# Moving the turning back of outputs, a set of score maxima and a norm between the gate steps of a gated feed-forward

## The chip, the cores and the metric

The kernel runs on one core of a Trainium2 chip. The metric is the device time of one execution, in microseconds (us); the time given for a kernel is the median of its runs.

## The reference

Two layers of a gated block work on eight sequences of 256 rows, 512 wide, with a context of 256 rows each. Cut to what matters:

```python
x = x + tanh(g_xattn[0]) * causal_attention(layernorm(x), ctx, ctx)      # 16 heads of 32
x = x + tanh(g_ffn[0]) * ffn0(layernorm(x))    # rms_norm(silu(gate) * up) @ w_proj, ternary weights
x = x + tanh(g_xattn[1]) * attention1(layernorm(x), ctx)   # projections, normed queries and keys
x = x + tanh(g_ffn[1]) * ffn1(layernorm(x))    # 8-bit activations, ternary weights
```

The change lies in the part that computes `ffn0` of layer 0 for all sequences, with the attention of layer 0 for the later sequences woven into it.

## The kernel before

The program has three parts. The first (until about 190 us) quantizes the weights of `ffn0`, computes keys and values for layer 1 and begins the attention of sequences 0 and 1. The second (about 190 to 728 us) runs `ffn0` of sequences 0 to 7 as eight blocks, b = 0 to 7. The third runs layer 1.

**A block.** `Feed0(b).chunks()` are 19 steps, one gate step to a sixteenth of the block's time. The last three project and overlap the next block's first three. A step n (called chunk n here) handles 128 rows and 256 hidden columns. TensorE (PE) computes `gu` in 32 matmuls. ScalarE (ACT) takes a tanh (L910) and VectorE (DVE) two products (L911, L912) that give `h` and free the PSUM bank of `gu`, of which there are two. ACT makes a half-precision copy (L916), DVE for even chunks or GpSimd (POOL) for odd ones the remainder `hs` (L299). ACT squares (L919), and POOL sums the squares into `acc` (L921). PE projects the chunk three steps later into `y` (one PSUM bank). After every eight chunks the row sum of squares `ssq` (PSUM tag `o`, one bank) gives a factor (L272 on DVE, L274 on POOL, L958 on DVE), and L963 adds `y` to the rows `x`.

**The feed-forward's entry.** `Feed0.ready()` has two steps. `norm` takes moments on DVE (L281, L282, L289, L272), `rs_r` on POOL (L274) and two normed tiles `y` on POOL (L294). `turn` casts the first `y` on ACT (L884), takes the remainder on DVE (L885) and issues a transposing DMA on the SP queue (L886), then does the same for the second. The tile `yp` between has one buffer:

```python
for i, y in enumerate(self.y):
    pp = f0.tile([P, 2, D], F16, tag="yp", name="yp", bufs=1)
    nc.scalar.copy(pp[:, 0], y)
    nc.vector.tensor_tensor(pp[:, 1], y, pp[:, 0], ALU.subtract)
    nc.sync.dma_start(out=self.xT[:, i], in_=pp.rearrange("p h d -> p (h d)"), transpose=True)
```

The first transposed half `xT[:, 0]` is read from chunk 0 of the sequence's block on, the second from chunk 8 on.

**The attention.** For the attention that is woven into block n (of sequence n + 2), `looks()` are four sets of scores with their negated maxima `nm` (L411, in layer 1 L419, on DVE), one set for four heads; then `parts`, which splits `nm` into three bf16 pieces `mz` in ten small POOL operations (L431, L434, L438); then `shift`, which turns `mz` on PE (`nt`) and copies it on DVE to `nT` (L449). `weighs()` computes the scores once more, adds `nT` in PSUM, takes exponentials `p` on ACT (L485) and multiplies by values (`o`, copied to `oT` by L519, sums on POOL by L522). `done()` turns the outputs back on PE (`back`, and `sums` in the PSUM bank `o`), inverts and multiplies on DVE (L584, two L590), and adds into `x` on DVE (two L600). `ready()` of the attention has a norm like the feed-forward's and `turn`, which turns `y` on PE (`turned`) with an ACT copy to `qT` (L348). Scores, `back`, `nt` and `turned` share a PSUM tag `s` of two buffers, two banks each.

**The weights of layer 1.** During blocks 0 to 2 ACT measures them (L1004). From about block 3 to 6 POOL scales and rounds them (L1028, L1032), DVE clips them (L1036) and SP stores them (L1037); loads are L993.

**What sets the order.** Every step has a place in time in blocks, written by hand: `at(b, (k, step))` places it at b + k/16, and `timeline` calls all steps by place. A step thus only emits its instructions in that order; the compiler's scheduler then orders them on each engine with a model of its own, and each engine runs its queue in order. PE's queue is held to the order of the calls (`pe.held`).

In block b, with the places in sixteenths, this stands between chunk 9 and the next block:

```
9.2   third scores; last weigh of the attention of sequence b + 1
10    chunk 10
10.4  fourth scores      10.8  parts
11    chunk 11
11.7  done (sequence b + 1: turn the outputs back, add to x)
12    chunk 12           12.4  feed-forward norm of sequence b + 1
13    chunk 13           13.4  feed-forward turn (casts, DMA)
14    chunk 14           14.6  shift (nt)
15    chunk 15           15.3  first exponentials
16    chunk 0 of block b + 1
```

Block 0 has `done` of sequence 1 at 1.3 and the feed-forward norm of sequence 1 at 4.4, outside this scheme. Blocks 5 and 6 also compute queries of layer 1 (`lin`) between chunks 12 and 14. In block 7 there is no `done` or norm for a next sequence.

Of the kernel before, what the change touches and what calls it, by code (L numbers as in the profile page):

```python
# [87 lines left out]
def flamingo_kernel(  # L88
# [39 lines left out]
    def banks(stack, name, **tags):  # L128
        pool = stack.enter_context(
            tc.tile_pool(name=name, bufs=1, space=PSUM, reuse_waits="tile")  # L130
        )
        part_ps.clear()
        part_ps.update({tag: (pool, n) for tag, n in tags.items()})
# [15 lines left out]
    def load_x(i, pool):  # L149
        xs[i] = pool.tile([P, D], F32, tag=f"x{i}", name=f"x{i}", bufs=1)  # L150
        nc.sync.dma_start(out=xs[i], in_=xf[i * P : (i + 1) * P, :])
# [44 lines left out]
    for g in range(DC):  # L196
        for i in range(2):
            at = SR * g + SR // 2 * i
# [163 lines left out]
    class Attention:  # L362
# [3 lines left out]
        n = 0  # L366
# [250 lines left out]
    def timeline(*jobs):  # L617

        steps = []
        for j, (a, z, job) in enumerate(jobs):  # L620
            steps += [(a + (z - a) * (n + 0.5) / len(job), j, step) for n, step in enumerate(job)]
        for _, _, step in sorted(steps, key=lambda e: e[:2]):
            step()

    def at(b, *steps):

        return [(b + n / 16, b + n / 16, [step]) for n, step in steps]
# [192 lines left out]
    with ExitStack() as part:  # L820
# [16 lines left out]
        jobs = []  # L837
# [162 lines left out]
    def measure1(u):  # L1000
        seen[0] += 1
        w = load1(u)
        a = q1.tile([P, QW], BF, tag="q", name="a1", bufs=2)
        behind(nc.scalar.activation(a, w, AF.Abs, accum_out=l1sum[:, u : u + 1]), block["A"])  # L1004
# [17 lines left out]
    def quantize1(u):  # L1022

        seen[1] += 1
        assert seen[0] == n1
        w = load1(u)
        _, dst, k = units1[u]
        ins = nc.gpsimd.tensor_scalar(w, w, wscale[:, k : k + 1], MAGIC, ALU.mult, ALU.add)  # L1028
        behind(ins, block["P"])
        hold1()  # L1030
        q = q1.tile([P, QW], BF, tag="q", name="q1", bufs=2)
        nc.gpsimd.tensor_scalar(q, w, 1.0, -MAGIC, ALU.mult, ALU.add)  # L1032

        def hold():
            q8 = q1.tile([P, QW], F8, tag="q8", name="q8", bufs=2)
            nc.vector.tensor_scalar(q8, q, 1.0, -1.0, ALU.min, ALU.max, saturate=False)  # L1036
            nc.sync.dma_start(out=dst, in_=q8.bitcast(U8))  # L1037

        left.append(hold)
# [83 lines left out]
    with ExitStack() as part:  # L1123
        banks(part, "ps1", o=1, gu=2, y=1)
        q1 = part.enter_context(tc.tile_pool(name="q1", bufs=1, side="right", reuse_waits="tile"))
        feed0 = [Feed0(b) for b in range(B)]

        def rows(b):
            load_x(2 * b, x2)
            load_x(2 * b + 1, x2)  # L1130

        jobs = [
            (0.5, 3.0, [lambda u=u: measure1(u) for u in range(n1)]),
            (3.05, 3.05, [scales1]),
            (3.1, 6.5, [lambda u=u: quantize1(u) for u in range(n1)]),
            (6.6, 6.6, [hold1]),
            (3.0, 3.0, [load_queries]),
        ]

        jobs += at(0, *zip((-5.0, -4.0), feed0[0].ready()), (1.3, *att0[1].done()))
        for b in range(B):
            jobs += at(b, *((k, step) for k, step in enumerate(feed0[b].chunks())))
            if b == 0:
                jobs += at(b, *zip((4.4, 5.4), feed0[1].ready()))
            elif b + 1 < B:
                jobs += at(b, *zip((12.4, 13.4), feed0[b + 1].ready()))
        for n, a in enumerate([*att0[2:], *att1[:2]]):  # L1150
            if n < B - 2:
                jobs += at(n, (-11.0, lambda n=n: rows(n + 2)))
                jobs += at(n, *zip((-4.8, *((1.4, 4.2) if n == 0 else (-2.4, 0.2))), a.ready()))
            else:
                jobs += at(n, *zip((-9.6, -7.6, -3.7, -2.6, -2.5, -2.4, 0.2), a.ready()))
            jobs += at(n, *zip((*((5.4, 7.2) if n == 0 else (1.2, 5.2)), 9.2, 10.4, 10.8, 14.6), a.looks()))
            if a is not att1[1]:
                jobs += at(n, *zip((15.3, 18.2, 19.2, 20.2, 22.2, 23.2, 24.2, 25.2), a.weighs()))
            if n < B - 2:
                jobs += at(n, (27.7, *a.done()))  # L1160
        timeline(*jobs)
    w0ctx.close()

# [197 lines left out]
    jobs = []  # L1361
    for b in range(B):
        first, second, a = feed1[2 * b], feed1[2 * b + 1], att1[b]
# [77 lines left out]
```

## Time and profile before

| | us |
|---|---|
| median of 3 runs (1191.4 to 1193.26) | 1191.43 |
| the profiled execution: its own time | 1192.33 |
| the profiled execution: span, first to last instruction | 1190.6 |
| PE busy (share of the span) | 1092.7 (92%) |
| DVE busy | 791.4 (66%) |
| ACT busy | 598.0 (50%) |
| POOL busy | 495.1 (42%) |

A line of the timeline gives the start and the length in us, the engine, the source line, the operation, the tile written and those read, partitions and shape, and in brackets the idle time before it and what ended that. A line of the waits gives who waited on whom: us in total, how often, the longest. A row of the windows gives a stretch, its length, the busy time of PE, PE's weight loads, DVE, ACT and POOL with instructions in parentheses, the granted TensorE clock, the DMA share and GB/s. One core runs, so its mean granted clock, 0.987, is the only one.

### The profile page before, as it was taken

How to read it: one execution, taken by the hardware profiler on the slowest of the kernel's cores; microseconds unless marked ns; L12 is line 12 of the kernel's file. 1: busy time of each engine (PE TensorE's matmuls, PEld its weight loads, DVE VectorE, ACT ScalarE, POOL GpSimd, SP SyncE). 2: the span in 40 equal slices, each digit the busy share in tenths (PEclk: the TensorE clock that was granted, in tenths of full speed). 3: DMA queues.
4: the chain of work that ended last, by engine and by line, in shares of the span. 5: the costliest groups of instructions: out<-in, count | busy, mean ns of one | idle time of the engine just before them, and what ended most of it. 6: DMA issues, size and time to landing. Idle time of an engine off the chain costs nothing.

```text
span 1190.6 us, 31314 instructions
## 1 busy us (share of the span) xinstructions
PE 1092.7 (92%) x13290; PEld 738.2 (62%) x13389; DVE 791.4 (66%) x1612; ACT 598.0 (50%) x1060; POOL 495.1 (42%) x792
## 2 busy tenths in 40 slices
PE   5899998999999989988999998998999999999987
PEld 1445446777777767776667775565656565656654
DVE  5686986745647375655656445687878787868585
ACT  3466554466665434344443542536363646464654
POOL 3112112543435475565645226544444444424250
PEclk9999999999999999999999999999999999999999
DMA  8444435523433233242311114011122122211212
GB/s 300 142 161 160 146 138 182 156 90 109 107 109 99 65 93 99 82 101 90 83 50 42 20 37 159 25 44 49 50 49 51 45 55 45 55 32 31 44 41 57
DMA packets 99469, 104.08 MB, mean 87 GB/s; under 512 B 60992, under 2 KB 72320, under 8 KB 99328
## 3 DMA queue, kind: packets, MB, share of 16 engines
q1 hardware_dynamic: 95728, 96.03, 27.8%
q10 hardware_dynamic: 3600, 6.03, 1.6%
q8 instruction: 105, 1.72, 0.6%
q14 instruction: 36, 0.29, 0.1%
HBM read 72.09 MB, written 15.73 MB: 74 GB/s over the span
## 4 chain that ended last, share of the span: by engine, by line
PE 34%; DVE 26%; POOL 17%; ACT 11%; issue 9%; DMA 3%; DVEq 0%; POOLq 0%; SPq 0%; ACTq 0%
PE gu L257 9%; PE o L257 6%; PE lin L257 6%; PE s L257 5%; DVE nm L419 4%; PE y L257 3%; ACT h L919 2%; POOL rs_r L274 2%; DVE h L912 2%; DMA xT<-yp 2%; DVE h L911 2%; PE py L257 2%; POOL hs L299 2%; POOL acc L921 2%; ACT hs L916 2%
## 5 line engine op out<-in xcount | busy, mean ns | idle before, releaser
L257 PE MATMUL gu<-xT,gu 128*128 128x128 f16 x4096 | 256.4, 222 | 10.5 <-DMA xT<-yp 6.8
L257 PEld LDWEIGHTS <-gu 128*128 128x128 bf16 x4096 | 238.9, 99 | 40.8 <-issue 18.0
L274 POOL TENSOR_TENSOR rs_r<-rs_t,mhalf 128x1 f32<-128x1 f32 (+1 forms) x88 | 61.9, 705 | 212.7 <-DVE rs_t L272 200.9
L257 PE MATMUL gu<-gv,zT 128*128 128x256 fp8e4 x1024 | 131.7, 275 | 6.0 <-ACT gv L1269 4.6
L921 POOL TENSOR_TENSOR acc<-acc,h 128x256 f32<-128x256 f32 x112 | 82.7, 739 | 114.9 <-ACT h L919 113.0
L257 PEld LDWEIGHTS <-zT 128*128 128x128 bf16 x1024 | 96.4, 98 | 51.8 <-issue 36.5
L1269 ACT COPY gv<-gu 128x512 f32<-128x512 f32 x128 | 74.0, 584 | 95.6 <-PE gu L257 75.3
L916 ACT CAST hs<-h 128x256 f16<-128x256 f32 x128 | 51.7, 404 | 138.7 <-DVE h L912 137.9
L257 PE MATMUL y<-pr,hs 128*128 128x512 bf16 x413 | 113.0, 381 | 6.2 <-DVE x L963 0.6
L485 ACT ACTIVATE p<-s 128x768 f32<-128x768 f32 (+1 forms) x128 | 109.5, 906 | 16.0 <-PE s L257 15.5
L911 DVE SCALAR_TENSOR_TENSOR h<-h,gu 128x256 f32<-128x256 f32 x128 | 53.2, 416 | 95.4 <-ACT h L910 95.2
L919 ACT ACTIVATE h<-h,hid 128x256 f32<-128x256 f32 x112 | 56.7, 508 | 67.4 <-POOL hs L299 41.3
L419 DVE TENSOR_REDUCE nm<-s 128x4 f32<-128x1024 f32 x64 | 75.7, 1219 | 21.8 <-PE s L257 21.8
L299 POOL TENSOR_TENSOR hs<-h,hs 128x256 f16<-128x256 f32 x64 | 43.7, 683 | 100.2 <-ACT hs L916 100.2
L1274 DVE SCALAR_TENSOR_TENSOR t<-t,gv 128x512 f32<-128x512 f32 x64 | 48.3, 754 | 45.9 <-ACT t L1273 45.9
L257 PE MATMUL s<-qT,kT 32*128 32x256 f32 (+1 forms) x1024 | 74.9, 372 | 2.6 <-DVE rs_t L272 1.6
L910 ACT ACTIVATE h<-gu 128x256 f32<-128x256 f32 x128 | 48.4, 378 | 50.4 <-PE gu L257 49.9
L257 PE MATMUL s<-kT,qT 32*128 32x256 f32 (+1 forms) x1024 | 68.9, 374 | 2.3 <-ACT p L485 1.9
L257 PE MATMUL lin<-wk,cT 128*128 128x512 f32 x128 | 61.0, 621 | 9.8 <-DMA wk<-in_k_wT_dram 9.8
L411 DVE TENSOR_REDUCE nm<-s 128x2 f32<-128x256 f32 (+1 forms) x128 | 62.8, 552 | 8.9 <-PE s L257 8.9
L257 PE MATMUL o<-p,v 128*32 128x256 f32 (+1 forms) x1024 | 61.7, 358 | 6.9 <-DVE x L1306 4.9
L522 POOL TENSOR_TENSOR oT<-oT 128x128 f32<-128x128 f32 x48 | 26.6, 555 | 98.4 <-ACT oT L519 98.4
(180 smaller groups left out, 2070.5 us busy)
## 6 DMA issues: line engine op xcount, KB each, us to landing
w<-in_gvT_dram SPq DMA_DIRECT2D x32, 512.0 KB
w<-in_guT_dram SPq DMA_DIRECT2D x16, 512.0 KB
w<-in_outT_dram SPq DMA_DIRECT2D x16, 512.0 KB
cT<-in_cxT_dram SPq DMA_DIRECT2D x8, 512.0 KB
x<-in_x_dram SPq DMA_DIRECT2D x16, 256.0 KB
kT<-in_cxT_dram SPq DMA_DIRECT2D x8, 512.0 KB
v<-in_cx_dram SPq DMA_DIRECT2D x8, 512.0 KB
kd<-k SPq DMA_DIRECT2D x8, 512.0 KB
```

The source lines that it names most:

```text
L257: return self.kept(nc.tensor.matmul(*args, **kwargs))
L274: nc.gpsimd.tensor_tensor(r[:, :n], t[:, :n], mhalf[:, :n], ALU.pow)
L299: (nc.vector if engine == "V" else nc.gpsimd).tensor_tensor(dst, a, b, op)
L411: nc.vector.tensor_reduce(nm[:, :, qb], s[j][:, :, at[qb] : at[qb] + to[qb]], AX.X, ALU.max, negate=True,)
L419: nc.vector.tensor_reduce(nm, s[j].rearrange("p r (q k) -> p r q k", q=2), AX.X, ALU.max, negate=True)
L485: exp[0] = nc.scalar.activation(self.p[j], s[j][:, :, 0:n], AF.Exp)
L910: block["A"] = nc.scalar.activation(h, gu[:, 0], AF.Tanh, scale=0.5 / UP0)
L911: nc.vector.scalar_tensor_tensor(h, h, 1.0, gu[:, 0], ALU.add, ALU.mult)
L916: nc.scalar.copy(hs[:, 0], h)
L919: nc.scalar.activation(sq, h, AF.Square, scale=hid[:, 1:2])
L921: block["P"] = nc.gpsimd.tensor_tensor(self.acc[i], self.acc[i], sq, ALU.add)
L1269: nc.scalar.copy(self.gv[:, :, k % 2, :], gu)
```

## The change

Places in time change, and nothing else. In blocks 1 to 6, `done` goes from 11.7 to 10.7, the feed-forward norm from 12.4 to 11.4 and its `turn` from 13.4 to 12.4. In all blocks the fourth scores go from 10.4 to 11.2 and `parts` from 10.8 to 11.6.

```diff
             elif b + 1 < B:
-                jobs += at(b, *zip((12.4, 13.4), feed0[b + 1].ready()))
+                jobs += at(b, *zip((11.4, 12.4), feed0[b + 1].ready()))
...
-            jobs += at(n, *zip((*((5.4, 7.2) if n == 0 else (1.2, 5.2)), 9.2, 10.4, 10.8, 14.6), a.looks()))
+            jobs += at(n, *zip((*((5.4, 7.2) if n == 0 else (1.2, 5.2)), 9.2, 11.2, 11.6, 14.6), a.looks()))
...
             if n < B - 2:
-                jobs += at(n, (27.7, *a.done()))
+                jobs += at(n, (26.7, *a.done()))
```

(The place 27.7 of the attention that is woven into block n is 11.7 of block n + 1.)

The order within a block is now: chunk 10, `done`, chunk 11, fourth scores, norm, `parts`, chunk 12, `turn`, chunk 13, chunk 14, `shift`, chunk 15.

## The prediction

> **What bounds the kernel now.** I read the page first: PE is busy 92% of the span, so time is lost only where PE stands still, and the list of what PE waited for comes next.
>
> ```profile
> PE gu L257 <- DMA xT<-yp: 6.8, 4, 2.8
> PE back L260 <- DVE nm L411: 1.0, 3, 0.3
> ```
>
> The first row is what the change can take away: four waits of the first gate matmuls of a block for the transposed rows `xT`. By window they are 0.93 us (block 1 into 2), 1.19 (2 into 3), 1.89 (3 into 4) and 2.79 (4 into 5). Blocks 5 and 6 show none. Next, PE's timeline where block 4 passes into block 5:
>
> ```profile
> 504.81 1.96 PE L257 MATMUL gu<-xT,gu 128*128 128x128 f16 x32 [0.55 <-DVE h L912]
> 507.47 0.28 PE L260 MATMUL nt<-ident_b,mz 128*128 128x128 bf16 x2
> 515.29 1.96 PE L257 MATMUL gu<-xT,gu 128*128 128x128 f16 x32 [2.79 <-DMA xT<-yp]
> 517.08 1.04 PE L260 MATMUL turned<-ident,y 128*128 128x128 f32 x8
> ```
>
> A gate step is 1.96 us of `gu` plus 0.8 to 1.0 of `y`. `nt` (the turned maxima) does not wait. Then POOL's timeline beside it:
>
> ```profile
> 498.06 0.20 POOL L431 TENSOR_SCALAR mz<-nm 128x16 bf16<-128x16 f32 x1
> 500.11 0.20 POOL L438 TENSOR_SCALAR mz<-nmr 128x16 bf16<-128x16 f32 x1
> 500.27 0.67 POOL L299 TENSOR_TENSOR hs<-h,hs 128x256 f16<-128x256 f32 x1
> 501.57 0.73 POOL L921 TENSOR_TENSOR acc<-acc,h 128x256 f32<-128x256 f32 x1 [0.62 <-ACT h L919]
> 502.27 1.55 POOL L1028 TENSOR_SCALAR w<-w,wscale 128x1024 f32<-128x1024 f32 x1
> 503.91 1.04 POOL L1032 TENSOR_SCALAR q<-w 128x1024 bf16<-128x1024 f32 x1
> 506.64 0.71 POOL L274 TENSOR_TENSOR rs_r<-rs_t,mhalf 128x2 f32<-128x2 f32 x1 [1.69 <-DVE rs_t L272]
> 508.04 1.52 POOL L294 TENSOR_SCALAR y<-x,ln_mv,rs_r 128x512 f32<-128x512 f32 x2
> ```
>
> The ten `mz`/`nmr` operations (`parts`) end at 500.3, so `nt` at 507.47 has 7.1 us of slack; the norm's `y` ends at 509.6. The chain of waits for this window runs through POOL, ACT and DVE in turn, not through PE. Last, ACT and DVE, where the transfer hangs:
>
> ```profile
> 510.13 0.68 DVE L885 TENSOR_TENSOR yp<-y,yp 128x512 f16<-128x512 f32 x1
> 515.26 0.62 ACT L884 CAST yp<-y 128x512 f16<-128x512 f32 x1 [2.83 <-DMA xT<-yp]
> 515.79 1.50 ACT L485 ACTIVATE p<-s 128x768 f32<-128x768 f32 x2
> ```
>
> `yp` has one buffer, so the second cast waits on ACT until the first transpose landed, 4.4 us after its issue at 510.84 (3.6 us in block 3). `turned` then takes the PSUM buffer that the first of the two `p` frees.
>
> **The change part by part.** Nothing is added or removed. In the built order of PE, `back`/`sums` and chunk 11 now stand ahead of the fourth scores in blocks 1 to 6; in blocks 0 and 7 only the scores go behind chunk 11. On DVE the four L411 leave their place ahead of the outputs' L584 to L600 and stand behind them and the first norm statistics. On POOL `parts` no longer stands ahead of hs(11): it comes behind hs(11) and acc(11), and it is cut in two by the norm's `rs_r` and its two `y`. That cut decides my forecast. I lay block 4 out again with the durations of before, PE reaching `back` at 493.2 as it then reached the scores.
>
> 1. `back` ends at 494.1. `sums` needs PSUM bank `o`, held by `ssq` until DVE reads it (L272, 494.45, behind an L1036): a new wait of 0.55. Behind it on PE stands chunk 11, 494.75 to 496.7, `y` to 497.6. The 0.34 of `back <- nm` is gone.
> 2. DVE is free for L584 at 496.62 (there the four L411 began). 0.39 and 1.20 for the two L590 give 498.2, which frees the buffer that the fourth scores need: PE waits 0.8, and chunk 12 starts at 499.4.
> 3. DVE goes on with L600 0.93, L911 0.45, L600 0.93, statistics 0.6, L912 0.45: the `h` of chunk 11 is done at 501.45, against 499.4. Chunk 12's `h` is done at 505.1 after statistics 0.6 and four L411 1.9, so chunk 14 starts at 505.15, 0.35 later than before.
> 4. POOL: hs(11) 502.0 to 502.65, ACT's square, acc 503.95, L1028 at 1.1 to 505.05, two `mz` 505.45, `rs_r` 506.15, L1032 507.2, two `nmr` 507.55, two `y` 509.05, acc 509.75, two `mz` 510.1, hs(13) 510.75, two `nmr` and two `mz` 511.6. PE is ready for `nt` at 507.95 and waits 3.7 us. Queued behind it are chunk 15, the first exponentials' scores and chunk 0: that starts at 516.65 against 515.29.
> 5. The transfer: first `y` 508.3 (0.5 earlier), cast on ACT 508.95, but DVE's L885 stands behind an L1036 that waits for L1032 (507.2), behind L911 and L912 of chunk 13 and behind two L281: 509.95 to 510.6. The issue on SP is 0.2 us earlier than before, not a step. It lands by 515.0, which the `nt` wait hides; the 2.79 is gone.
> 6. The second cast still blocks ACT until 515.0, now with chunk 15's tanh queued behind it. `p` also stands behind the square of chunk 15, which needs POOL's hs(15), which stands behind the attention norm: acc(13) 512.2, L1028 513.3, `rs_r` 514.4, acc 515.1, L1032 516.1, two `y` 517.6, hs(15) 518.3, square 518.85, first `p` read by 519.7. `turned` starts at 519.7 against 517.08: **+2.6**.
>
> Block 3 has the same rows 69.5 us earlier: `turned` at 450.2 against 447.88, **+2.3**. Blocks 1 and 2 have no L1028/L1032. There `parts` ends at 307.1 and `nt` waits 1.0; chunk 0 of block 2 starts at 312.1 (before 312.06, of which 0.93 waiting). POOL's attention norm is late (its L272 stands behind the copy of `nt`: 309.7, two `y` until 313.0), hs(15) 314.35, first `p` by 315.75: `turned` against 313.92 gives **+1.8**. Block 2 lies 62.5 us later: 378.25 against 378.06, **+0.2**, because the old 1.19 and a wait of 1.27 ahead of `turned` go. In blocks 5 and 6 two stretches of 3.6 us of `lin` lie ahead of `nt` and cover `parts`. Their new waits at `sums` and scores (1.35 in block 5, none in block 6), less two `back` waits of 0.3 and part of the 0.75 of `s <- nT`, are **+0.2**. In blocks 0 and 7 `parts` comes one step later (about 2.8 us) under some 5 us of cover: 0. Uncovered, that step would cost up to 2.8 each. In layer 1 PE's order is unchanged; stores and `uT` transposes change places on SP. The only wait there of `py` on `uT` is 2.4 us: I take 0, bounds -2 and +2.
>
> What a wait of 3.7 us does to the clock, rows of before bound:
>
> ```profile
> 444.80:448.00 3.20, 3.12 (x33) 3.12 (x34) 0.85 (x2) 2.53 (x4) 3.20 (x4) 0.59 0.14 30
> 515.20:517.00 1.80, 1.71 (x31) 1.72 (x32) 1.03 (x1) 1.74 (x3) 1.80 (x3) 1.00 0.00 0
> ```
>
> After the wait of 1.89 the granted clock (third number from the end) was 0.59, and 32 `gu` took 3.21 instead of 1.96; after the 2.79 it was 1.00. So the price is 0 or 1.25 per stall. I take 0, since `turned` waits until 519.7 anyway and chunk 0 would end at 519.9 with it.
>
> The Trainium skill, "TensorE: Matmul & The Clock Gate", section "What's actually happening", says that an idle window of about 3.4 us drops the clock to half. By it both 3.7 us waits would cool PE and the sum would be 2.5 higher; the row at 444.8 shows a drop after a shorter gap, so here the rows decide.
>
> Sum: 2.6 + 2.3 + 1.8 + 0.2 + 0.2 = **+7.1 us** on the profiled execution's 1192.33 (span 1190.6 and 1.7 around it) = 1199.4. That execution was 0.9 above the median 1191.43, so I predict 1198.5.
>
> **Rivals.** (a) Faster: the norm is early enough and `nt` finds its parts. For it: all four `xT` waits are under 2.8 us, less than one step. Against: POOL's order puts `y` into the middle of `parts`. It decides if the last `mz` of blocks 3 and 4 is done by 508, 3.6 us ahead of my layout. Then 6.8 and 0.7 of `back` waits go, less new waits at scores and `sums` of about 2.7: -4.8, 1186.6; down to 1184 without them. (b) No change: `nt` waits as laid out, but squares and `p` do not slip. Then `turned` moves with chunk 0: +1.4 and at most +2.3 in blocks 4 and 3, 0 and -1.5 in blocks 1 and 2, in all +1 to +2: about 1193. That is also what follows if the issue of `xT` moves by just 0.2. (c) Worse: the clock drops after both stalls and SP's new order holds up `uT`: +2.5 and +2, 1203.
>
> **How the numbers follow.** My layout 0.56, (a) 0.17, (b) 0.17, (c) 0.10. About 0.2% (2.4 us) is what a measurement of this kernel can tell from no change. Faster is (a), 0.17; same is (b), 0.17; slower is mine and (c), 0.66. The range goes from 1188, inside (a), to 1203.5, just above (c).
>
> **What would show it.** Right: PE's waits list `nt <- POOL mz`, about 1 us in blocks 1 and 2 and 3 to 4 in blocks 3 and 4; `gu <- xT` is gone; `turned <- ACT p` grows to 1 or 2 us a time; the first `xT` issue of block 4 comes no more than 1 us sooner against chunk 14. Wrong: `nt` without a wait, or a last `mz` ahead of the two `y`; then (a) holds.

## The result, and the profile after

The changed kernel takes 1209.07 us (median of 4 runs, 1208.45 to 1210.92) against 1191.51 for the kernel before: a ratio of 1.0153 with a 95% interval of 1.0137 to 1.0169. That is 17.6 us slower; the forecast was 7.1 slower. The direction was right, the size not, and the time lies above the range. The profiled execution has a span of 1207.6 us (before 1190.6).

First, what PE waited for (waits of PE, changed kernel; total us, times, longest):

```profile
PE nt L260 <- POOL mz L438: 10.7, 4, 4.2
...
PE gu L257 <- DMA zT<-zq: 3.4, 2, 2.0
...
PE s L257 <- DVE nT L449: 2.5, 2, 2.3
```

The first row is the predicted wait of the turned maxima; in order of time its four parts are 1.11, 1.11, 4.22 and 4.22. No row `gu <- DMA xT` is left, and none of `back`. Two rows the prediction had not foreseen: `s <- nT` was 0.7 and is 2.5, and `gu <- zT` in layer 1 was one wait of 1.3 and is two of 3.4 in all. (`sums <- rs_t`, which it had foreseen, is 1.4.)

PE's timeline where block 4 passes into block 5 (start, us, operation, and in brackets the wait ahead of it):

```profile
499.02 0.30 PE L260 MATMUL sums<-ident,oT 128*128 128x128 f32 x1 [0.61 <-DVE rs_t L272]
...
515.93 0.45 PE L260 MATMUL nt<-ident_b,mz 128*128 128x128 bf16 x2 [4.22 <-POOL mz L438]
516.17 3.53 PE L257 MATMUL gu<-xT,gu 128*128 128x128 f16 x32
...
524.50 1.06 PE L260 MATMUL turned<-ident,y 128*128 128x128 f32 x8
```

PE stands still for 0.61 us ahead of `sums`, as laid out (0.55), and for 4.22 us ahead of `nt`. Chunk 15 then takes 3.53 in place of 1.96, and `turned` comes at 524.50, 7.42 later than before. POOL's timeline beside it:

```profile
508.84 0.38 POOL L431 TENSOR_SCALAR mz<-nm 128x16 bf16<-128x16 f32 x2
509.18 0.71 POOL L274 TENSOR_TENSOR rs_r<-rs_t,mhalf 128x2 f32<-128x2 f32 x1
509.87 1.05 POOL L1032 TENSOR_SCALAR q<-w 128x1024 bf16<-128x1024 f32 x1
510.88 0.84 POOL L434 TENSOR_TENSOR nmr<-nm,mz 128x16 f32<-128x16 f32 x2
511.72 1.52 POOL L294 TENSOR_SCALAR y<-x,ln_mv,rs_r 128x512 f32<-128x512 f32 x2
...
515.67 0.37 POOL L438 TENSOR_SCALAR mz<-nmr 128x16 bf16<-128x16 f32 x2
```

This is the order that the prediction laid out: two `mz`, `rs_r`, L1032, two `nmr`, the two `y` of the norm, and the last `mz` at 516.0.

To see where the 17 us arise, I take the starts of the same PE operations in both traces, `turned` where a block ends and later `nt`, and note by how much the shift grows from one mark to the next:

| stretch | shift grows by | forecast |
|---|---|---|
| up to block 1 | -0.2 | 0 |
| block 1 / 2 / 3 / 4 | +1.24 / -0.16 / +2.78 / +3.74 | +1.8 / +0.2 / +2.3 / +2.6 |
| blocks 5 and 6, to `nt` of block 7 | +4.1 | +0.2 |
| from there into the second sequence of layer 1 (`turned` at 870.63) | +3.6 | 0 |
| from there to the last tile | +1.9 | 0 |

Blocks 1 to 4 give 7.6 of a forecast 6.9. The miss lies behind them: 4.1, 3.6 and 1.9.

### The profile page after: what moved, and what is told of

Read it like the earlier page. It is cut to its first block, busy times and chain, and to the rows that moved or that the text cites. A ratio compares the mean times of both kernels' runs of the same rounds, so it can differ in the third digit from the quotient of the medians.

```text
span 1207.6 us, 31403 instructions
## 1 busy us (share of the span) xinstructions
PE 1104.6 (91%) x13389; PEld 742.5 (61%) x13389; DVE 790.7 (65%) x1612; ACT 597.1 (49%) x1060; POOL 497.1 (41%) x792
## 4 chain that ended last, share of the span: by engine, by line
PE 34%; DVE 25%; POOL 19%; ACT 10%; issue 9%; DMA 2%; POOLq 0%; DVEq 0%; SPq 0%; ACTq 0%
PE gu L257 10%; PE lin L257 6%; PE o L257 6%; PE s L257 5%; DVE nm L419 4%; PE y L257 3%; POOL rs_r L274 3%; DVE h L912 2%; POOL acc L921 2%; ACT h L919 2%; POOL hs L299 2%; PE py L257 2%; DVE h L911 2%; POOL w L1028 2%; POOL q L1032 2%
## 5 line engine op out<-in xcount | busy, mean ns | idle before, releaser
L257 PE MATMUL y<-pr,hs 128*128 128x512 bf16 x512 | 132.5, 382 | 0.9 <-DVE x L963 0.9
L921 POOL TENSOR_TENSOR acc<-acc,h 128x256 f32<-128x256 f32 x112 | 81.8, 731 | 117.3 <-ACT h L919 110.2
L919 ACT ACTIVATE h<-h,hid 128x256 f32<-128x256 f32 x112 | 56.7, 507 | 71.6 <-POOL hs L299 46.0
```

The lines of the kernel that those rows point to most:

```text
L257: return self.kept(nc.tensor.matmul(*args, **kwargs))
L919: nc.scalar.activation(sq, h, AF.Square, scale=hid[:, 1:2])
L921: block["P"] = nc.gpsimd.tensor_tensor(self.acc[i], self.acc[i], sq, ALU.add)
```

## The experiments

The kernel before took 1191.0 to 1191.6 us (median) beside each of them. "By the marks" means the shift of the same PE operations against the trace of before.

**The parts alone.** The first run moves only the fourth maxima and the parts (against the kernel before):

```diff
-  9.2, 10.4, 10.8, 14.6), a.looks()
+  9.2, 11.2, 11.6, 14.6), a.looks()
```

> The fourth scores and parts stand behind chunk 11 as in the change; outputs, norm and turn stay where they were. On POOL parts is whole and ahead of the norm's two y, and the instructions of layer 1 stand in the order of before. Theory A (the loss in blocks 1 to 4 is POOL's cut parts, so that nt waits): no wait of nt over 1 us, the xT waits of 6.8 us stay, 1190 to 1195 us. Theory B (what costs is that the fourth scores and their maxima come late at all): nt waits 2 us or more in blocks 3 and 4 here too, 1198 us or more.

Measured 1213.77 us, ratio 1.0184 [1.0168, 1.0199]. `nt` does not wait, as theory A had it, but the time is 23 us up, a miss for both theories: `back <- nm` 6.1, `gu <- h` 7.4 and `y <- x` 5.3 are longer or new, and 3.3 of the `xT` waits stay. With the maxima late, the outputs and products behind them on DVE hold PE up, as POOL does in the whole change.

The second moves only the outputs and the norm:

```diff
-  (12.4, 13.4), feed0[b + 1].ready()
+  (11.4, 12.4), feed0[b + 1].ready()
-  (27.7, *a.done())
+  (26.7, *a.done())
```

> Outputs, norm and turn a step sooner; fourth scores and parts stay ahead of chunk 11. Both theories: nt does not wait, the xT waits are gone (-6.8 us). Price: back now stands right behind the fourth scores on PE and needs the PSUM buffer that their first two L411 free; by the rows of before these end 3.4 us after PE gets there in blocks 3 to 5 and 1.8 us in blocks 1 and 2, 2 in block 6, so back <- nm waits some 15 us in all. 1199 us, range 1190 to 1203.

Measured 1209.93, ratio 1.0156 [1.0137, 1.0175]. The wait is as expected:

```profile
PE back L260 <- DVE nm L411: 13.8, 5, 3.5
```

It is the largest of PE's waits in that trace, the `xT` waits are gone, and still the time is 11 us above the forecast and outside its range. The granted clock of PE, which the forecast did not count, goes with that: between block 1 and `nt` of block 7 its mean is 0.962 in this trace and 0.986 in that of before, which leaves out some 12 us more of PE's work (one minus the mean clock, times the length of the stretch). So the two halves cost about 23 and 19 us, and together 17.6: they partly undo each other, and no half is a gain.

**POOL's order alone.** The third run keeps the change, but the parts come at 11.3 and the norm's two `y` are held behind the last of them (against the changed kernel):

```diff
-  9.2, 11.2, 11.6, 14.6), a.looks()
+  9.2, 11.2, 11.3, 14.6), a.looks()
-  nc.gpsimd.tensor_scalar(y, t, ...)
+  behind(nc.gpsimd.tensor_scalar(y, t, ...), last_mz)
```

> The change, with the places of the scores and parts at 11.2 and 11.3 and the two y of the feed-forward's norm held behind the last operation of parts on POOL. The rest of the order of blocks 3 and 4 stays, but layer 1's instructions fall back into the order of before. Theory A: nt waits 1.6 us instead of 4.2 in blocks 3 and 4 and under 1 in blocks 1 and 2. For layer 1, theory C (its 5.5 us of loss come from the order of its instructions on DVE, POOL, SP): they go, 1196 us. Theory D (they come from entering layer 1 late or from the clock): they stay, 1201 to 1204 us.

Measured 1205.66, ratio 1.0114 [1.0097, 1.0132]:

```profile
PE turned L260 <- POOL acc L922: 6.0, 2, 3.5
...
PE turned L260 <- ACT p L486: 3.5, 3, 2.0
...
PE nt L260 <- POOL mz L439: 3.2, 2, 1.6
PE gu L257 <- DMA xT<-yp: 3.0, 3, 2.0
```

(The lines of this run are numbered one higher.) The waits for the multipliers fall from 10.7 to 3.2, so POOL's cut `parts` do make them. But 3.0 of `xT` come back and `turned` waits 9.5 in place of 3.2: by the marks the time up to `nt` of block 7 is longer than in the changed kernel (+14.4 against +11.5). POOL's work has to be done in either order. The time lies above the ranges of both C and D; by the marks C is right, as layer 1, back in the order of before, adds nothing behind that mark (-0.7).

**Blocks alone.** The change in some blocks, the old places in the others:

```diff
-  (11.4, 12.4), feed0[b + 1].ready()
+  (11.4, 12.4) if b in blocks else (12.4, 13.4), feed0[b + 1].ready()
-  9.2, 11.2, 11.6, 14.6), a.looks()
+  9.2, *((11.2, 11.6) if n in blocks else (10.4, 10.8)), 14.6), a.looks()
-  (26.7, *a.done())
+  (26.7 if n + 1 in blocks else 27.7, *a.done())
```

> The whole change in blocks 3 and 4 alone; blocks 0, 1, 2, 5, 6, 7 have the places of before. Layer 1's order is nearly that of the changed kernel. Theory A: nt waits 4.2 us twice, turned of the attention norm in block 5 comes 6.5 us late, as the changed kernel adds in these two blocks. Theory C: layer 1, from the nt of block 7 to the end, is 5 us longer than before, 472 us instead of 467. Together with 1.5 us of slow clock in block 5: 1204 us. Theory D says the same for a late entry, theory B the same for the blocks.

> The whole change, but in blocks 5 and 6 of layer 0 alone; layer 1 then has the instruction order of the kernel before. In the changed kernel the marks of the turned tiles go from +7.4 us at the end of block 4 to +11.5 us at the norm of block 7, so blocks 5 and 6 cost 4.1 us there. Theory A (these blocks cost by their own moved steps): about 4 us here too, 1195 us (1194 to 1197). Theory B (the cost is carried over from the waits of blocks 3 and 4, by the clock or a queue that is behind): nothing here beyond the 0.2 us of the prediction, 1191.5 us (1190.5 to 1192.5).

> The whole change in blocks 1 and 2 of layer 0 alone; layer 1 has the order of before. The prediction gave these blocks 2.0 us, the marks of the changed kernel 1.1 us (1.24 and -0.16). If blocks add up: 1192.5 us (1191.5 to 1193.5), with two waits of some 1.1 us of the norm's transposes for its multipliers. If what a block costs depends on the blocks around it: 1196 us or more, or below 1191.

> The whole change in blocks 1 to 4 of layer 0; blocks 5, 6, 0 and 7 keep the old places, and layer 1 has an order close to that of the changed kernel. All theories: +7.5 us at the end of block 4, with the four waits of the norm for its multipliers (1.1, 1.1, 4.2, 4.2 us). Theory A (blocks 5 and 6 cost by their own steps) keeps +7.5 us to the start of layer 1; theory B (carried over) rises to about +11 us there. Then, if layer 1 costs 5.5 us by its instruction order, the end stands 5 us further back (A: 1204 us, B: 1207 us); if it does not, 1198.5 us (A) or 1202.5 us (B).

| blocks | time, us | ratio | marks: after block 4 | `nt` of block 7 | second sequence of layer 1 |
|---|---|---|---|---|---|
| 3, 4 | 1197.75 | 1.0059 [1.0037, 1.0081] | +6.8 | +5.9 | +7.1 |
| 5, 6 | 1198.39 | 1.0063 [1.0046, 1.0079] | -0.4 | +3.6 | +3.7 |
| 1, 2 | 1191.08 | 0.9998 [0.9989, 1.0007] | +2.3 | -0.4 | -0.4 |
| 1 to 4 | 1202.03 | 1.0088 [1.0073, 1.0103] | +7.5 | +8.4 | +11.3 |
| all | 1209.07 | 1.0153 [1.0137, 1.0169] | +7.6 | +11.7 | +15.3 |

The marks here are taken from each trace's own start of block 1, as executions begin up to 1.6 us apart from that of the kernel before. They come from one execution each, and the executions of one kernel differ: with blocks 3 and 4 from 1196.70 to 1202.44, and with 5 and 6 the traced one took 1195.42 and the other three 1198.1 to 1199.2. Of the times forecast, none was met: 1204 became 1197.75, 1194 to 1197 became 1198.39, 1191.5 to 1193.5 became 1191.08, and 1204 (theory A with a loss in layer 1) became 1202.03, near the 1202.5 of theory B without one. So it is the marks that tell the theories apart: +8.4 at `nt` of block 7, where B had about 11. Blocks 1 and 2 cost nothing alone: their 1.1 us (marks at the end of block 2) are gone by the end of layer 0. That is in part luck of the clock, as PE's waits between block 1 and `nt` of block 7 are 3.2 us longer than before and its granted clock leaves out 3.4 us less. Blocks 3 and 4 give 6.8, in the changed kernel 6.5. Blocks 5 and 6 alone give 4.0, with blocks 1 to 4 in their old places, so theory A holds: these blocks cost by their own moved steps. Where they keep their old places, `nt` of block 7 stands 0.9 later than the end of block 4 had left it (blocks 1 to 4) or 0.9 earlier (blocks 3 and 4), not 4.

**The norm's step alone left out.**

```diff
-  (11.4, 12.4), feed0[b + 1].ready()
+  (12.4, 13.4), feed0[b + 1].ready()
```

> The norm for the feed-forward keeps its old places (12.4 and 13.4); the outputs' transposes and the third and fourth maxima are moved as in the change. The two programs differ in few places of the order, so if the norm's place does almost nothing beside the outputs' place: 1209 us (1207.5 to 1210.5). If the norm's step is what makes the waits for its multipliers: these waits (10.7, 4.0 and 4.2 us in the changed kernel) go, and the time falls to 1200 us or less.

Measured 1202.68, ratio 1.0100 [1.0085, 1.0115]: neither. The waits for the multipliers are the same (10.6 in all), so the norm's place is not what makes them; POOL's order is the same up to block 4, and in block 5 the `y` come later between the parts. The 6.6 us that this trace's span (1201.0) is shorter are 1.4 of an earlier start, 0.4 up to `nt` of block 6, 1.7 from there to the second sequence of layer 1, and 3.1 behind that, where DVE, POOL and SP of the two kernels have the same order. The last part goes with the granted clock, as the end of the next part shows over all traces.

**The clock.** Read in windows of 1 us, the granted clock falls to 0.50 for 3.4 us at a time, sometimes twice in a row: between 60 and 1190 us 8 times in the trace of before, 11 times after, and in the latter twice more from 1195.3 on. Each such spell begins in or soon behind a wait of PE of 1.6 to 4.2 us. The prediction took the price of a spell as 0. To test this, PE fills the waits with work that nobody uses.

```diff
 def shift(self):
     t = pair((P, 2, P), BF, name="nt")
+    for k in range(64):                      # first and second run, blocks 3 and 4
+        pe.transpose(t[:, k % 2, :], ident_b, ident_b)
 ...
+jobs += at(b, (5.1, warm))   # second to fourth run, bank of chunk 6: 24 to 32 matmuls of 128x128
 def hidden(self, i, c):
+    spin(gu, {3: 14, 4: 26, 5: 40}[b])       # fourth run, chunk 0
```

> The changed kernel, in which PE does 64 more 128x128 transposes of the identity into the bank of the turned maxima in blocks 3 and 4, just before the transposes that wait there for POOL's last piece (4.22 us each). They fill the wait (about 3.9 us of it) and give nothing that is used. Theory A (a wait leaves PE at half clock for 3.4 us, which costs 1.7 us each time; the spells at 440 to 448 and at 516 come from these two waits): the spells go and the time falls by 3.4 to 5.1 us, to 1205 us (1203.5 to 1206.5). Theory B (what the prediction took: the clock costs nothing there, because the next tile waits for the exponentials anyway): 1209 us (1208 to 1211).

> As the run before, and in blocks 4 and 5 also 32 more matmuls (2.0 us) into the bank of the sixth chunk's gate product, ahead of the second scores, where PE waits 2.2 and 2.3 us for the exponentials and runs at half clock after it (spells at 475 and 546 to 554). Theory A: three more spells go, up to 5.1 us more, 1201 us (1198.5 to 1204). Theory B: 1209 us (1208 to 1211).

> The kernel before with such filling matmuls alone: 24, 30, 32 and 28 into the bank of the sixth chunk in blocks 3, 4, 5 and 6, where PE waits 1.8, 2.1, 2.3 and 1.9 us for the exponentials. The order of all engines is that of before apart from them. Spells of half clock follow these waits at 401, 540 and 616. Theory A: three spells of 1.7 us go, 1186.5 us (1185 to 1188.5). Theory B: no gain, or 0.2 us lost where the filling runs over the wait, 1191.5 us (1190.5 to 1192.5). Theory A2 (the spells only move to the next wait): 1190 us.

> As the run before, and 14, 26 and 40 filling matmuls also in the first gate step of blocks 3, 4 and 5, where PE waits 1.2, 1.9 and 2.8 us for the transposed rows; a spell of half clock follows the second of these waits at 445. Theory A: one spell more goes, 1185 us (1183 to 1187.5). Theory B: 1191.5 us (1190.5 to 1193).

| filled | time, us | ratio |
|---|---|---|
| after: `nt` of blocks 3, 4 | 1208.27 | 1.0140 [1.0126, 1.0154] |
| after: also chunk 6 of blocks 4, 5 | 1207.68 | 1.0138 [1.0123, 1.0154] |
| before: chunk 6 of blocks 3 to 6 | 1191.22 | 0.9995 [0.9986, 1.0004] |
| before: also chunk 0 of blocks 3 to 5 | 1193.41 | 1.0019 [1.0009, 1.0029] |

Theory A of these runs, mine at that point, falls. PE's timeline of the first, block 4 into 5 (its lines are numbered up to five higher):

```profile
510.39 3.74 PE L260 MATMUL nt<-ident_b 128*128 128x128 bf16 x64
514.78 0.40 PE L260 MATMUL nt<-ident_b,mz 128*128 128x128 bf16 x2 [0.66 <-POOL mz L441]
515.01 1.95 PE L257 MATMUL gu<-xT,gu 128*128 128x128 f16 x32
...
523.56 1.06 PE L260 MATMUL turned<-ident,y 128*128 128x128 f32 x8 [1.54 <-POOL acc L926]
```

The filling takes 3.74 of the wait, the clock stays at 1.00, and chunk 15 is back at 1.95. But `turned` now waits 1.54 for POOL's sum, where it did not wait before. From chunk 15 to `turned` it is 8.55 us here and 8.33 in the changed kernel, with chunk 15 at half clock. In the third run the spells at 401, 445, 540 and 616 are gone (two come up in layer 1); `nt` of block 7 is 2.4 us earlier, layer 1 1.9, and the median 0.4, which its interval does not tell from no change. So in layer 0 most of a slow spell lies beside work of other engines that PE would wait for anyway.

The fourth run has an answer for layer 1. Its `nt` of block 7 is 0.5 us earlier than in the kernel before, but its instruction order in layer 1 has changed with the filling, and there it loses 3.4 us.

At the end of the program it is otherwise. From the last `nt` to the last tile, PE's waits are 11.3 us in all both before and after, and yet this stretch is 89.0 us before and 90.8 after. In the three traces whose clock stays at 1.00 there it is 87.1, with one spell 87.3 to 88.2 (the kernel with the norm left is one of these, at 87.8), with two 88.1 to 89.0 (before), with three 89.7 to 91.0, with four 90.8 (after). Here a spell goes with some 1 us of time (a straight line through the 17 traces gives 1.03).

**What remained: blocks 5 and 6, and layer 1.** For the first, the trace of the changed kernel shows a chain. ACT, block 5 into 6:

```profile
592.54 0.62 ACT L884 CAST yp<-y 128x512 f16<-128x512 f32 x1 [1.96 <-DMA xT<-yp]
593.07 0.50 ACT L919 ACTIVATE h<-h,hid 128x256 f32<-128x256 f32 x1
```

The square L919 stands behind the second cast, which waits for the one buffer of `yp`. In the kernel before the square came first:

```profile
580.62 0.51 ACT L919 ACTIVATE h<-h,hid 128x256 f32<-128x256 f32 x1 [0.98 <-POOL hs L299]
583.28 0.62 ACT L884 CAST yp<-y 128x512 f16<-128x512 f32 x1 [2.16 <-DMA xT<-yp]
```

POOL, DVE and PE of the changed kernel go on from there:

```profile
593.65 0.82 POOL L921 TENSOR_TENSOR acc<-acc,h 128x256 f32<-128x256 f32 x1 [2.32 <-ACT h L919]
...
595.66 1.05 POOL L1032 TENSOR_SCALAR q<-w 128x1024 bf16<-128x1024 f32 x1
596.67 0.80 POOL L274 TENSOR_TENSOR rs_r<-rs_t,mhalf 128x2 f32<-128x2 f32 x1
```

```profile
596.74 0.69 DVE L1036 TENSOR_SCALAR q<-q 128x1024 fp8e4<-128x1024 bf16 x1 [1.14 <-POOL q L1032]
...
597.68 1.41 DVE L766 SCALAR_TENSOR_TENSOR lin<-lin,rs_r,rnq 128x512 f32<-128x512 f32 x2
599.01 0.28 DVE L449 COPY nT<-nt 128x256 bf16<-128x256 bf16 x1
```

```profile
599.34 0.29 PE L257 MATMUL s<-mask_k_m,mask_k_f 32*128 32x64 bf16 x14 [2.27 <-DVE nT L449]
```

The sum L921 waits for the square, L1032 and `rs_r` for POOL, L1036 for L1032, and `nT` stands behind L1036 and two L766 on DVE. PE waits 2.27 in place of 0.75. If the cast did not wait, the square would be early. So `yp` gets two buffers, in the pool of layer 1's query tiles, where there is room:

```diff
-  pp = f0.tile([P, 2, D], F16, tag="yp", name="yp", bufs=1)
+  pp = q1.tile([P, 2, D], F16, tag="yp", name="yp", bufs=2)
```

> Blocks 5 and 6 alone changed, as in the fifth run, and the tile yp has two buffers, so that the second cast on ACT does not wait for the first transpose. POOL keeps the layer-1 order of before. Theory Y (the chunk's square stands on ACT behind that waiting cast; POOL's sum, L1028, L1032 and rs_r stand behind the square, and DVE's L1036, L766 and nT behind these, so PE waits 2.27 us for nT in place of 0.75): the wait for nT falls under 1 us, the two blocks cost 1 to 2.5 us by the marks in place of 4.1, and the time is 1193 us (1190.5 to 1195.5). Rival Z (nT is late because POOL's parts and norm now stand together, whatever ACT does): the wait stays at 2 us or more, the blocks cost about 4 us, 1195 to 1198.5 us as in the fifth run.

> The kernel before with two buffers for yp and nothing else; its layer 1 has POOL's order of the changed kernel. In layer 0 theory Y expects little (no square stands behind the second cast there in blocks 5 and 6; in blocks 1 to 4 the waits for the transposed rows stay, as these are for the first half): the marks at the end of layer 0 stand between -2 and 0. In layer 1 theory C (POOL's order there makes PE wait 2.0 to 2.4 us for the transpose of zq and costs about 3 us) expects that wait and +3 us: 1193 us (1191 to 1195). If layer 1's cost comes from what layer 0 hands over, it is not there: 1190.5 us (1189 to 1192).

> The changed kernel with two buffers for yp; layer 1 has POOL's order of the changed kernel. Theory Y: of the 4.1 us of blocks 5 and 6 about 2 us go, and the 4.2 us waits of blocks 3 and 4 for the multipliers stay: 1206 us (1203.5 to 1208). Rival Z: 1209 us (1207.5 to 1211).

All three reach block 1 later, by 5.7, 5.6 and 7.3 us, with a wait `gu <- xT` of 6.8 to 8.0 us ahead of block 0: `yp` is first written 8 to 9 us later there. By the code its new place is taken by the first part's tiles until then. This is in their times (1203.79, ratio 1.0108 [1.0093, 1.0123]; 1197.57, 1.0045 [1.0029, 1.0061]; 1211.66, 1.0168 [1.0152, 1.0183]) and is taken off the marks.

In the first, the wait for `nT` is gone, as theory Y said, but the two blocks cost 5.3 us by the marks, more than with one buffer and far from the forecast 1 to 2.5. PE waits elsewhere, and comes to `nT` later by that wait:

```profile
587.63 5.40 PE L257 MATMUL lin<-wq,xT 128*128 128x512 f32 x8 [2.37 <-DVE lin L756]
```

The adding of the query bias (L756) that frees that bank stands on DVE behind two L885, which wait for ACT's casts, and these for POOL's `y` (583.71 to 585.39). The whole change (third run) is the cleaner test: from `lin` to `nt` PE's waits are those of the changed kernel, and `nT` is copied 3.8 us after `nt` in place of 5.0, so PE waits 1.1 for it in place of 2.3. So the waiting cast makes 1.2 us of the wait for `nT`. It is not shown that this is worth anything: blocks 5 and 6 cost 2.7 there in place of 4.1, but PE's waits over them are 12.0 us in all against 11.2 (`sums` alone waits 1.5 in place of 0.2), and the granted clock leaves out 1.7 us of PE's work in place of 3.4. That POOL's norm and parts, now side by side, are what is left is argued from these traces, not shown by a run of its own.

For layer 1 the second run decides. Its layer 0 has the places of before and reaches `nt` of block 7 1.2 us early; the order in layer 1 is that of the changed kernel on POOL, and nearly so on DVE. Its waits of PE have this row, 2.3 at the first feed-forward:

```profile
PE gu L257 <- DMA zT<-zq: 3.6, 2, 2.3
```

and it loses 2.7 us from `nt` of block 7 to the second sequence. Over all traces: nine have that order on POOL (the changed kernel, the runs with blocks 3 and 4, with 1 to 4, with the norm left, the two fillings of the changed kernel, the second filling of before, and the last two with two buffers); all wait 1.8 to 2.4 us for `zT` there and lose 1.1 to 4.5 us over this stretch, 2.9 in the middle. The other seven, whose POOL takes the first `z` early as before, have no such wait and lose 0.0 to 0.5, one of them 1.2. The spread goes with the clock. With that order, no spell of half clock in the stretch goes with a loss of 1.1, two with 2.7 to 3.6, three with 3.4, four with 4.5; without it, one with 0.0 to 0.2, two with 0.3 and 0.5, three with 1.2 (the kernel before has one). DVE's order changes in the same nine, so no run has POOL's change alone.

## Why the prediction was right and wrong

**Right: blocks 1 to 4 and their mechanism.** Step 4 put POOL's last `mz` of block 4 at 511.6, with `nt` waiting 3.7 us. PE reaches `back` 4.2 us later than laid out (497.38 against 493.2), which makes it 515.8; measured 516.0, and a wait of 4.22. The layout of block 4 gave +2.6 and measured +3.74, that of block 3 +2.3 and +2.78, blocks 1 and 2 +2.0 together and +1.08. The sum, 6.9 forecast and 7.6 measured, is confirmed by the run with these four blocks (7.5). That it came out so near is in part luck, as blocks 3 and 4 were taken 1.6 too low and blocks 1 and 2 0.9 too high.

**Right: the transfer.** It is issued 5.6 us after the start of chunk 14, before 6.0: 0.4 sooner, far from the step that the words of the change suggest.

**Right in place, wrong in the waits foretold: `turned`.** It was laid out at 519.7, with the 4.2 us 523.9, and came at 524.50. But its waits for ACT and POOL did not grow to 1 or 2 us a time (3.2 in all, before 3.5), as the half clock of chunk 15 fills that time; in the filled run the wait of 1.54 shows.

**Right for the stalls it was made for: the price 0 of a stall's clock.** The clock did fall in or behind both long waits (at 441.0 and 516.1). The reason for the price, "`turned` waits until 519.7 anyway and chunk 0 would end at 519.9 with it", is what the filled run shows. Rule and row differ here. "TensorE: Matmul & The Clock Gate" of the Trainium skill, section "What's actually happening", lets the clock fall after an idle window of about 3.4 us. The traces show spells of that length, but behind waits of 1.75, 1.88 and 2.27 us too, and none behind one of 2.79; and of the 2.5 us that the rule would add, the filled run gets nothing back by `turned` of block 4 (8.55 against 8.33). For the rest of the program the price of 0 does not hold, at the end above all.

**Wrong: the term of blocks 5 and 6, +0.2.** The step said that two stretches of `lin` cover `parts`, that new waits at `sums` and scores are 1.35, and that part of the 0.75 of `s <- nT` goes. Covering was right: `nt` does not wait there. New waits of 1.5 in block 5 (`lin <- ln_mv` 0.5, `s <- oT` 0.5, `s <- rs_t` 0.3, `sums` 0.2) against 1.35 were right in sum, though a third of them is at `lin`. But `s <- nT` grew to 2.27: I followed this on PE only, and not the second cast on ACT, the square behind it, and POOL and DVE behind that, as I had done for block 4. Behind block 5 there are new waits too: `y <- x` 0.9 and `lin <- nm` 0.3. Measured +4.1, and 4.0 alone. Over the stretch PE's waits are 7.6 before and 11.2 after, at the same mean clock of 0.98; `nT` is 1.7 of these 3.6. So it is the largest part, not the whole.

**Wrong: layer 1 at 0 with bounds of 2.** I had compared PE's order and SP's there and looked for the cost at `uT`. The order that changed and cost is POOL's, and with it DVE's, in the first feed-forward of layer 1. In the kernel before, POOL takes the first row tile's `z` (L1226) ahead of the second tile's `rs_r` (745.50); in the changed one `rs_r` (758.03) comes first, and the second `z` comes ahead of the residual sum. These are the rows of the first `z`, before and after:

```profile
744.28 1.27 POOL L1226 TENSOR_TENSOR z<-yr,rnw 128x512 f32<-128x512 f32 x1
```

```profile
759.06 1.26 POOL L1226 TENSOR_TENSOR z<-yr,rnw 128x512 f32<-128x512 f32 x1
```

Counted from `turned` (742.48 and 754.87), `z` starts 2.4 us later. The transposing DMA of `zT` (SP's queue, changed kernel) is issued 10.75 us after `turned` at 754.87; before it was 6.53 (749.01 after 742.48):

```profile
765.62 4.59 SPq L1248 DMA_TRANSPOSE zT<-zq  x2
```

Of these 4.2 us, 2.4 are the later `z`, and 2.0 are two DVE operations that now run beside POOL's (L1231 0.46 and 1.32, L1234 0.43 and 1.52); the rest nearly cancels. They are 2.0 more than lay covered: PE waits 2.04 for `zT`, and a spell of half clock begins 0.6 us behind that wait's end. Measured +3.6 over the stretch: PE's waits grow by 1.6 in all, and the granted clock leaves out 3.4 in place of 1.7 us of PE's work.

**Wrong: nothing for the end, and with it the clock's price of 0 there.** The stretch behind the second sequence gives another +1.9, nearly all of it behind the last `nt`. PE's waits there are the same in sum: `ut <- uq` 3.0 (before 1.2), but `py <- uT` 1.0 (before 2.4). The granted clock is not: two spells in a row, from 1195.3, lie on PE's last chain of work, from `ut` to the last tile, which takes 7.6 us where it took 5.1. The kernel with the norm left in place has the same order there, no spell on that chain, takes 5.1 for it, and gains 1.2 instead. Why the spells fall so in one kernel and not in the other was not foreseen; that they go with the time is read from all traces, not from a run that changes the clock there alone.

Rival (c) had the right side and 1203, with SP's order in layer 1 as one of its two costs. Its other cost, the clock, did fall behind both stalls, but gave nothing back when it was filled. Its chance of 0.10 was too low: that layer 1 gets another order could be read before the run, and I priced only the queue I had looked at.

## What to carry to other kernels

When a step is moved, lay out every place where it recurs with the queues of all engines, not just the place where it shows most; the block that looks covered on PE may be the one that pays through ACT, POOL and DVE. When a scheduler orders the rest, compare its order on each engine over the whole program: here half of the loss beyond the forecast (3.6 and 1.9 of 10.5) arose in code that the change never names. And where an engine off the list of bounds is nearly as tight as PE, taking one wait away brings up the next; none of the versions tried beats the kernel before.

## What the runs showed of the hardware

The granted clock of PE falls in whole spells of 3.4 us at 0.50. Here is one in the changed kernel (windows; the third number from the end is the granted clock): PE's wait and the spell.

```profile
512.00:515.90 3.90, 0.00 (x0) 0.00 (x0) 3.60 (x10) 1.73 (x5) 3.90 (x10) 1.00 0.57 171
515.90:520.00 4.10, 4.07 (x37) 3.77 (x38) 1.32 (x3) 1.62 (x4) 4.10 (x6) 0.58 0.29 55
```

The clock of 0.58 over 4.1 us is 1.7 us of PE's work. Five such spells less in layer 0 of the changed kernel left 0.4 us less at `nt` of block 7, four less in the kernel before 2.4.

Where a spell falls can be read from the traces too. All changes of the granted clock in a trace lie on one raster of 3.413 us. In the trace of before, from 60 us on, PE was busy for 0.22 to 0.45 of each stretch of the raster that was followed by a spell, and for 0.51 or more of every other stretch at full clock; after, it was 0.04 to 0.53 ahead of a spell and 0.47 or more elsewhere. So a wait counts by how much of one stretch it takes: the wait of 1.89 us before `gu` at 444.88 lies in one (PE busy 0.45), that of 2.79 at 515.29 is cut in two at 513.61 (0.67 and 0.51), and no spell follows it.

And some of DVE's operations grow when POOL works beside them. The rounding of `zq` (L1234) took 0.43 us before and 1.52 in the changed kernel, where POOL ran the residual sum L1237 from 764.04 to 765.31 beside it (DVE 764.08 to 765.60). Of the 32 L1234 of the two traces, the three with such a sum or product of POOL (L1237, L1226) beside them took 1.42 to 1.52 and ended 0.28 us behind it; the other 29 took 0.41 to 0.43. In the changed kernel this growth is 1.1 of the 4.2 us by which `zT` is issued later.
